# A four-stage image kernel: one move and one normalisation to ScalarE, loads and stores to other queues, a product in two column halves

## The chip, the cores and the metric

The kernel runs on one core of one Trainium2 chip. The metric is the device time of one execution in microseconds. All arithmetic is in fp32. TensorE, VectorE, ScalarE and GpSimd work in parallel, and each takes its own instructions in order; SyncE (SP in the profile) issues DMAs. The ScalarE queue can issue DMAs too.

## What is computed

An image x of 48 channels and 128 by 128 pixels passes through four layers. Each takes a group-normalised input (16 groups of 3 channels) and adds its result to x.

```python
# 0: attention over all 16384 pixels, one head of 48 channels
q, k, v = split(depthwise3x3(qkv_w @ gn(x)))
x = x + proj_w @ (softmax(l2norm(q) @ l2norm(k).T * temperature) @ v)
# 1: four recurrent sweeps (down, up, right, left), each row or column plus a 5-tap conv of the one before
x = x + sweeps(gn(x))
# 2: 8x8 patches: q and k are multiplied in the frequency domain, layer-normed, gated by v
q, k, v = split(depthwise3x3(w_hidden @ gn(x)))
x = x + w_out @ (v * layernorm(irfft2(rfft2(q) * rfft2(k)))) + b_out
# 3: selective scan over 4096 tokens (2x2 windows) of 192 features, 192 states
delta = softplus(softplus(tokens @ W_dt.T + b_dt) + b_dt)
h = exp(delta * A) * h + (delta * u) * B        # for every token
x = x + (h @ C + D * u) * sigmoid(1)
```

## The kernel before

**Attention** (`attend`) works on chunks of 512 queries (32 chunks) against 64 tiles of keys. For each tile, `scores` makes four products on TensorE (pass by pass, eight records, 64x64 positions of the array) and one exp on ScalarE (L48 `e<-s`); `sums` adds tile j into `acc`, two tiles behind (`BEHIND = 2`). TensorE and ScalarE run in an order written out by hand: the `InOrder` wrapper chains every instruction given to `act` or `pe` to the one before it, and all of these are recorded under its line, L48. VectorE is not chained in this stage. At the end of a chunk, `Finish` copies `acc` to `o` on ScalarE, adds the two halves into `both` on VectorE (L366), moves partitions 64 to 127 of it to a tile `second` (L368), adds (L370, `y`), takes the reciprocal of the row of sums (L373, `rec`) and spreads it over 48 partitions with three DMAs (L376, `recs`). `Finish.result` multiplies, adds the residual, takes statistics and stores the chunk; it stands after tile 6 of the next chunk in the order, and directly after the last chunk.

**Sweeps** begin with GpSimd memsets of borders of the image buffer (L592 to L608; the largest, L604, covers 32 partitions by 16512 elements), the group statistics (L71 to L87) and a ScalarE normalisation (L617).

**The patch stage** (`patch_conv`) works on 32 groups of four image rows in a software pipeline written out by hand for TensorE, ScalarE and VectorE. In the order of one round: `columns` (24 passes `pc`), `turn` of three groups back (four transposes `po<-ident,y`), `others`, `keys` (`f`), `back` of two groups back (`po<-k,gm`, then mean and difference on VectorE and a square on ScalarE), `leave` of three groups back (the product with `wout`, then bias and residual in one VectorE instruction), `gate` of two groups back (variance, root, multiplication on VectorE; three GpSimd multiplications and additions, L893 to L895), `queries` and `count`. The three kinds of `po` share two PSUM buffers.

**The scan** begins with `token_stats`, which leaves scale and offset in `so`. `scan` loads weights on two queues, makes `a = -exp(A_log)`, and prepares the first 1024 tokens in `first`: it normalises two parts of 512 tokens, projects them (`both`, whose accumulators are the two PSUM buffers named `dA`), runs softplus twice, and stores `rep` (delta and delta times u) and `yu` in DRAM. Activation functions that need another table make a load of 1.28 us (ACT_TABLE_LOAD). The main loop has 32 rounds a chunk of 1024 tokens, with three steps each. A step loads `du` and `dt` from `rep` on SP (L1484), multiplies on GpSimd (L1489, `h<-du,bt`), makes three exps on ScalarE (`dA<-dt,a`) and three scans on VectorE (L1496). TensorE contracts `h` with `cw` into `y`. The tiles `cw` are placed from `ct` by six ScalarE copies after `first`. Later chunks are prepared in small portions within the loop.

DMAs complete on eight semaphores that are used in turn over both queues; a DMA whose semaphore is still in use waits in its queue.

Of the kernel before, what the change touches and what calls it, by code (L numbers as in the profile page):

```python
# [19 lines left out]
F32 = mybir.dt.float32  # L20
F16 = mybir.dt.float16
AF = mybir.ActivationFunctionType
ALU = mybir.AluOpType
# [3 lines left out]
C = 48  # L27
H = W = 128
N = H * W
CH = 512  # L30
GAP = 49
SIGMOID_1 = 0.7310585786300049
# [63 lines left out]
def rows(ap, n=W):  # L96
    return ap.rearrange("c (r w) -> c r w", w=n)
# [209 lines left out]
@with_exitstack  # L307
def attend(ctx, tc, xq, k, v, x1, absT, st, ins):

    nc = tc.nc
    act, pe = InOrder(tc, nc.scalar), InOrder(tc, nc.tensor)
    NQ = N // CH
    KT = N // 2 // 128
    BEHIND = 2

    ep = ctx.enter_context(tc.tile_pool(name="l0_e", bufs=BEHIND + 3))  # L320
    sp = ctx.enter_context(tc.tile_pool(name="l0_b", bufs=2))
    ps_s = ctx.enter_context(tc.tile_pool(name="l0_ps", bufs=3, space=PSUM))
    ps_a = ctx.enter_context(tc.tile_pool(name="l0_pa", bufs=1, space=PSUM))


    sides = [slice(0, 64), slice(64, 128)]
    quarters = [(part, half, to) for part in sides for half, to in enumerate(sides)]

    def scores(c, j):
        s = ps_s.tile([128, 2, CH], F32, name="s")  # L330
        for part, half, _ in quarters:
            b = 64 * half
            pe.matmul(
                s[part, half, :],
                lhsT=k[b : b + GAP, j * 128 + part.start : j * 128 + part.stop],
                rhs=xq[b : b + GAP, c * CH : (c + 1) * CH],
                start=True,
                stop=True,
            )
        e = ep.tile([128, 2, CH], F32, name="e")  # L340
        act.activation(e, s, AF.Exp, scale=absT)
        return e

    def sums(acc, j, e):

        for part, half, to in quarters:
            pe.matmul(
                acc[to, part.start // 64, :],
                lhsT=v[part, half * KT + j, :],
                rhs=e[part, half, :],  # L350
                start=(j == 0),
                stop=(j == KT - 1),
            )

    class Finish:


        def __init__(self, c, acc):
            self.c = c
            self.cols = slice(c * CH, (c + 1) * CH)  # L360
            self.xres = sp.tile([C, CH], F32, name="xres")
            nc.sync.dma_start(self.xres, ins["x"][:, self.cols])
            o = sp.tile([128, 2, CH], F32, name="o")
            act.copy(o, acc)
            both = sp.tile([128, CH], F32, name="both")
            nc.vector.tensor_add(both, o[:, 0], o[:, 1])  # L366
            second = sp.tile([64, CH], F32, name="second")
            nc.vector.tensor_copy(second, both[64:128])  # L368
            self.y = sp.tile([64, CH], F32, name="y")
            nc.vector.tensor_add(self.y, both[0:64], second)  # L370

            rec = sp.tile([64, CH], F32, name="rec")
            nc.vector.reciprocal(rec[32:64], self.y[32:64])  # L373
            self.rec = sp.tile([C, CH], F32, name="recs")
            for i in range(0, C, 64 - C):
                nc.sync.dma_start(self.rec[i : i + 64 - C], rec[C:64])  # L376

        def result(self):
            y = self.y[0:C]
            nc.vector.tensor_mul(y, y, self.rec)  # L380
            nc.vector.tensor_add(xq[0:C, self.cols], y, self.xres)
            nc.vector.bn_stats(st[:, self.c, :], xq[0:C, self.cols])
            nc.sync.dma_start(x1[:, self.cols], xq[0:C, self.cols])

    waiting, finish, acc = [], None, None
    for c in range(NQ):
        for j in range(KT):
            waiting.append((c, j, scores(c, j)))

            if c and j == BEHIND:  # L390
                continue
            while len(waiting) > BEHIND:
                n, i, e = waiting.pop(0)
                if i == 0:
                    acc = ps_a.tile([128, 2, CH], F32, name="acc")
                sums(acc, i, e)
                if i == KT - 1:
                    finish = Finish(n, acc)
            if c and j == BEHIND + 4:
                finish.result()  # L400
    for n, i, e in waiting:
        sums(acc, i, e)
    Finish(NQ - 1, acc).result()


@with_exitstack
# [304 lines left out]
def patch_conv(ctx, tc, xq, other, x3, const, ins):  # L711

    nc = tc.nc
    act, pe, dve = (InOrder(tc, e) for e in (nc.scalar, nc.tensor, nc.vector))
    ident = const["ident"]
    C2, C6 = 2 * C, 6 * C
# [4 lines left out]
    sp = ctx.enter_context(tc.tile_pool(name="l2_s", bufs=2))  # L721
    ps_c = ctx.enter_context(tc.tile_pool(name="l2_pc", bufs=4, space=PSUM))
    ps_f = ctx.enter_context(tc.tile_pool(name="l2_pf", bufs=1, space=PSUM))
    ps_o = ctx.enter_context(tc.tile_pool(name="l2_po", bufs=2, space=PSUM))
# [18 lines left out]
    wout = wp.tile([C2, C], F32, name="wout")  # L743
    nc.sync.dma_start(wout, ins["l2_wout"])
    bout = wp.tile([C, 1], F32, name="bout")
# [158 lines left out]
        act.copy(yts[g], pt)  # L904

    def leave(g):
        pw = ps_o.tile([C, CH], F32, name="po")
        pe.matmul(
            pw, lhsT=wout, rhs=yts.pop(g).rearrange("c r w -> c (r w)"), start=True, stop=True
        )  # L910
        xc = xq[0:C, g * CH : (g + 1) * CH]
        dve.scalar_tensor_tensor(xc, pw, bout, xc, ALU.add, ALU.add)

    def count(g):
        dve.bn_stats(const["st"][:, g, :], xq[0:C, g * CH : (g + 1) * CH])
# [53 lines left out]
def scan(ctx, tc, x3, const, ins, out):  # L969
# [7 lines left out]
    nc = tc.nc  # L977
# [3 lines left out]
    C2 = 2 * C  # L981
# [26 lines left out]
    def load(name, shape, eng):  # L1008
        t = wp.tile(shape, F32, name=name)
        eng.dma_start(t, ins[f"l3_{name}"])  # L1010
        return t

    wdt = load("wdt", [C2, 2, 2, C2], nc.sync)
    bdt = load("bdt", [C2, 2], act)
    wb = load("wb", [C2, 2, 3, 128], nc.sync)
    bb = load("bb", [128, 3], act)
    wc = load("wc", [C2, 2, 3, 128], nc.sync)
    bc = load("bc", [128, 3], act)
    a = load("a", [128, 3, Q], nc.sync)
    dp = load("dp", [C2, 2], act)  # L1020
    sel = load("sel", [128, BK, 8], act)
    act.activation(a, a, AF.Exp)
    nc.vector.tensor_scalar_mul(a, a, -1.0)
    plus = ident[0:C2, 0:C2]
    minus = wp.tile([C2, C2], F32, name="minus")
    nc.scalar.mul(minus, plus, -1.0)
    sig = wp.tile([128, 128], F32, name="sig")
    nc.scalar.mul(sig, ident, SIGMOID_1)


    cw = wp.tile([128, 3, LC // BK, 2 * BK], F32, name="cw")
# [10 lines left out]
    def prepare(ci):  # L1042
# [9 lines left out]
        def first():  # L1052
# [8 lines left out]
            for part, x in enumerate(us):  # L1061
                xi = rows(const["x3"][:, part, :]).rearrange("c i (j b) -> c i j b", b=2)
                xo = x.rearrange("c b (i j) -> c i j b", j=64)
                if part == 0:
                    act.activation(
                        xo, xi, AF.Identity, bias=so[:, 1:2], scale=so[:, 0:1]
                    )
                else:
                    nc.vector.tensor_scalar(xo, xi, so[:, 0:1], so[:, 1:2], ALU.mult, ALU.add)

            def both(lhsT, m):
                t = ps_a.tile([128, LC], F32, name="dA")
# [19 lines left out]
            for again in range(2):  # L1092
                for b in range(2):
                    split(b, dd[:, b, 0] if again else both(lambda i: wdt[:, i, b, :], C2))
                for b in range(2):
                    act.activation(e[:, b], e[:, b], AF.Exp, scale=-1.0)
                    nc.vector.tensor_scalar_add(w[:, b], e[:, b], 1.0)
                for b in range(2):
                    act.activation(ln[:, b], w[:, b], AF.Ln)

                    nc.vector.scalar_tensor_tensor(
                        w[:, b], w[:, b], 1.0, e[:, b], ALU.subtract, ALU.subtract
                    )
                    nc.vector.tensor_sub(e[:, b], dd[:, b, 1], w[:, b])
                if again == 0:
                    for k in range(2):
                        take_both(bt[:, k], both(lambda i: wb[:, i, k, :], 128), bb[:, k : k + 1])
                for b in range(2):
                    nc.vector.tensor_add(dd[:, b, 0], e[:, b], ln[:, b])
            take_both(bt[:, 2], both(lambda i: wb[:, i, 2, :], 128), bb[:, 2:3])  # L1110
            for b in range(2):
                for part, x in enumerate(us):
                    cols = slice(part * L, (part + 1) * L)
                    nc.vector.tensor_mul(dd[:, b, 1, cols], dd[:, b, 0, cols], x[:, b, :])
                for i in range(2):
                    half = slice(i * C, (i + 1) * C)
                    nc.sync.dma_start(rep_by[i][:, b], dd[half, b])
            for k in (2, 0, 1):
                take_both(ct[:, k], both(lambda i: wc[:, i, k, :], 128), bc[:, k : k + 1])
            for part, x in enumerate(us):  # L1120
# [2 lines left out]
                        w[:, b, part * L : (part + 1) * L], x[:, b], AF.Copy, scale=dp[:, b : b + 1]  # L1123
                    )
            for i in range(2):
                nc.sync.dma_start(yu_by[i][:, :, 0:LC], w[i * C : (i + 1) * C])

        def accumulator():
            return ps_p.tile([128, L], F32, name="pp")
# [609 lines left out]
```

## Time and profile before

| what | value |
|---|---|
| median of three runs | 7612.05 us (7606.72 to 7613.94) |
| the profiled execution | 7615.01 us |
| its span, first to last instruction | 7613.2 us |
| granted TensorE clock, mean | 0.885 |
| busy TensorE, VectorE, ScalarE, GpSimd | 80%, 45%, 58%, 37% |
| attention, first convolution to last chunk | 0 to about 3778 us |
| sweeps, with their start | 3778 to about 4490 us |
| patch stage, with its start | 4490 to about 4884 us |
| scan, with its start | 4884 to 7613 us |

The page gives busy time for each engine and a chain that ended last, followed back from the last instruction to what released each step. Since the four stages follow one another, a share of the whole span says little of a seam between two of them; the timeline of a window shows each instruction with its start, its duration, and in brackets the idle time of its engine before it with what ended that idle time. A busy TensorE is modelled at its ends, and work on GpSimd is rough.

### The profile page before, as it was taken

Reading aid. Unit: us, or ns where it says so; the run is one execution under the profiler, and the core shown is the slowest. Engines: PE = TensorE matmul, PEld = TensorE weight load, DVE = VectorE, ACT = ScalarE, POOL = GpSimd, SP = SyncE. Lnnn points to the kernel's source line nnn. Section 1 sums busy time; section 2 is a strip of 40 time slices with the busy share of each in tenths; the row PEclk is TensorE's granted clock in tenths of the full one; section 3 lists DMA queues with packets and bytes.
Section 4 is the critical chain, followed back from the end, with each engine's and each line's share of the span. In section 5 each row is a group of like instructions: output and inputs, shape, how many; then the busy total and the mean of one; then the engine's idle time right before and its main releaser. Section 6 shows DMA issues by size and latency. Waiting matters only on the chain.

```text
span 7613.2 us, 203122 instructions
## 1 busy us (share of the span) xinstructions
PE 6126.1 (80%) x93692; PEld 3179.7 (42%) x93692; DVE 3405.3 (45%) x2498; ACT 4389.0 (58%) x4835; POOL 2791.8 (37%) x574
## 2 busy tenths in 40 slices
PE   7999999999999999999888889745545545554555
PEld 3333333333333333333367765334434433434444
DVE  8300000000000000000122234499999999999998
ACT  2566666666666666666525003367666666666665
POOL 0000000000000000000000022299999999999998
PEclk9999999999999999999999999867767766676667
DMA  3000000000000000000000011166656666666776
GB/s 66 9 3 4 4 3 4 4 4 3 4 4 4 3 4 4 3 4 4 3 1 17 1 32 37 31 163 169 159 160 163 157 160 153 167 162 162 177 182 149
DMA packets 182349, 484.83 MB, mean 64 GB/s; under 512 B 35859, under 2 KB 67778, under 8 KB 179506
## 3 DMA queue, kind: packets, MB, share of 16 engines
q1 hardware_dynamic: 175167, 466.19, 24.2%
q8 instruction: 734, 12.03, 0.7%
q10 hardware_dynamic: 6323, 5.59, 0.3%
q14 instruction: 125, 1.02, 0.0%
HBM read 428.03 MB, written 22.02 MB: 59 GB/s over the span
## 4 chain that ended last, share of the span: by engine, by line
PE 60%; DVE 24%; issue 6%; POOL 3%; ACT 2%; DMA 2%; SPq 0%; DVEq 0%; ACTq 0%; POOLq 0%
PE s L48 23%; PE acc L48 23%; DVE h L1496 21%; PE p L672 6%; POOL h L1489 3%; PE pc L48 3%; PE y L48 3%; DVE xb L48 1%; DVE xa L48 1%; PE po L48 1%; DMA du<-rep 1%; PE f L48 1%; ACT dA L48 1%; PE pp L48 0%; ACT L48 0%
## 5 line engine op out<-in xcount | busy, mean ns | idle before, releaser
L48 ACT ACTIVATE e<-s,absT 128x1024 f32<-128x1024 f32 x2048 | 2279.3, 1115 | 1217.2 <-PE s L48 1217.2
L1489 POOL TENSOR_TENSOR h<-du,bt 128x3072 f32<-128x3072 f32 (+1 forms) x386 | 2559.5, 6675 | 96.7 <-DMA du<-rep 69.7
L48 PE MATMUL s<-xa,xb 49*64 49x512 f32 x16384 | 2137.3, 589 | 10.6 <-DVE xb L271 10.6
L48 PE MATMUL acc<-e,xb 64*64 64x512 f32 x16384 | 2135.4, 588 | 0.0
L1496 DVE TENSOR_TENSOR_SCAN h<-dA,carry,h 128x1024 f32<-128x1024 f32 x864 | 1940.2, 2322 | 41.0 <-ACT dA L48 27.3
L48 ACT ACTIVATE dA<-dt,a 128x1024 f32<-128x1024 f32 x1152 | 1287.2, 1118 | 877.4 <-DVE h L1496 865.2
L48 PE MATMUL y<-h,cw 128*32 128x48 f32 x49152 | 891.7, 244 | 956.6 <-issue 501.6
L366 DVE TENSOR_TENSOR both<-o 128x512 f32<-128x512 f32 x32 | 22.1, 692 | 3192.8 <-ACT o L48 3192.8
L608 POOL MEMSET xa<- 48x128 f32 x1 | 0.3, 327 | 3523.5 <-PE acc L48 3523.5
L48 PEld LDWEIGHTS y<-h,cw 128*32 128x32 f32 x49152 | 801.1, 139 | 1081.7 <-issue 664.8
L48 PEld LDWEIGHTS s<-xa,xb 49*64 49x64 f32 x16384 | 650.5, 132 | 1123.2 <-issue 583.4
L48 PEld LDWEIGHTS acc<-e,xb 64*64 64x64 f32 x16384 | 649.7, 132 | 1112.4 <-issue 1089.5
L1496 DVE TENSOR_TENSOR_SCAN h<-dA,h 128x1024 f32<-128x1024 f32 x288 | 636.0, 2270 | 41.3 <-ACT dA L48 30.4
L48 PE MATMUL yz<-ev,sel 128*8 128x48 f32 x4096 | 192.4, 260 | 270.6 <-ACT ev L48 269.0
L48 PEld LDWEIGHTS yz<-ev,sel 128*8 128x8 f32 x4096 | 162.2, 106 | 327.8 <-ACT ev L48 306.4
L672 PE MATMUL p<-xb,l_w 112*112 112x129 f32 x1524 | 236.4, 291 | 41.8 <-DVE xb L48 41.7
L672 PE MATMUL p<-xa,l_w 112*112 112x129 f32 x1524 | 232.2, 288 | 41.8 <-DVE xa L48 41.8
L693 POOL TENSOR_TENSOR xb<-xb,xa 48x2048 f32<-48x2048 f32 (+2 forms) x10 | 44.6, 4459 | 561.7 <-DVE xa L48 561.7
L672 PEld LDWEIGHTS p<-xb,l_w 112*112 112x112 f32 x1524 | 184.3, 179 | 93.6 <-DVE xb L48 93.6
L655 ACT COPY xa<-xb 48x128 f32<-48x128 f32 x256 | 107.3, 419 | 197.2 <-issue 138.8
L672 PEld LDWEIGHTS p<-xa,l_w 112*112 112x112 f32 x1524 | 180.6, 176 | 93.2 <-DVE xa L48 93.2
L48 PE MATMUL pc<-wt,xa 128*128 128x288 f32 x768 | 199.7, 418 | 7.5 <-DMA xa<-xa 7.5
(187 smaller groups left out, 3345.7 us busy)
## 6 DMA issues: line engine op xcount, KB each, us to landing
du<-rep SPq DMA_DIRECT2D x768, 256.0 KB
dt<-rep SPq DMA_DIRECT2D x768, 256.0 KB
rep<-dd SPq DMA_DIRECT2D x24, 192.0 KB
yd<-ys ACTq DMA_DIRECT2D x256, 12.0 KB
rest<-xa SPq DMA_DIRECT2D x90, 38.0 KB
band<-band SPq DMA_DIRECT2D x8, 414.4 KB
xa<-in_x_dram SPq DMA_DIRECT2D x8, 384.0 KB
rest<-band SPq DMA_DIRECT2D x96, 32.0 KB
```

What stands on the lines that cost most here:

```text
L48: ins = method(*args, **kwargs).ins
L366: nc.vector.tensor_add(both, o[:, 0], o[:, 1])
L608: nc.gpsimd.memset(b[64:K, lines, E + W - 1 : E + W], 0.0)
L655: nc.scalar.copy(u[at : at + C, :, y], t[0:C, E + h, E : E + W])
L672: nc.tensor.matmul(p, lhsT=w[0:K, which, i, :], rhs=state[0:K, 2 * i : 2 * i + L], start=False, stop=(i == 2),)
L693: nc.gpsimd.tensor_add(xr, xr, u[0:C, x : x + xr.shape[2], E : E + H].rearrange("c w h -> c h w"),)
L1489: nc.gpsimd.tensor_mul(h[:, p, ks], du.unsqueeze(1).to_broadcast([128, ks.stop - ks.start, LC]), r["bt"][:, ks],)
L1496: nc.vector.tensor_tensor_scan(h[:, p, k, :], dA, h[:, p, k, :], carry[:, i, k : k + 1] if ci else 0.0, ALU.mult, ALU.add,)
```

## The change

In `attend`, the move of the upper half of `both` goes from VectorE to ScalarE. A new method `divide` holds it with the addition, the reciprocal and its DMAs; it stands after tile 4 of the next chunk, and `result` after tile 8 in place of tile 6. In `patch_conv`, the output product is made in two halves of 256 columns, which go to PSUM partitions 0 to 47 and 64 to 111; two VectorE instructions add bias and residual. In `scan`, all loads go on SyncE; the exp of `a`, its sign and two scaled identities go to a function `tables` that is called in the middle of the first preparation; both first normalisations are on ScalarE; of the four first `rep` stores, two go on the ScalarE queue, and so do the two first `yu` stores.

```diff
-            both = sp.tile([128, CH], F32, name="both")
-            nc.vector.tensor_add(both, o[:, 0], o[:, 1])
+            self.both = sp.tile([128, CH], F32, name="both")
+            nc.vector.tensor_add(self.both, o[:, 0], o[:, 1])
+
+        def divide(self):
             second = sp.tile([64, CH], F32, name="second")
-            nc.vector.tensor_copy(second, both[64:128])
+            act.copy(second, self.both[64:128])
             self.y = sp.tile([64, CH], F32, name="y")
-            nc.vector.tensor_add(self.y, both[0:64], second)
+            nc.vector.tensor_add(self.y, self.both[0:64], second)
...
-            if c and j == BEHIND + 4:
+            if c and j == BEHIND + 2:
+                finish.divide()
+            if c and j == BEHIND + 6:
                 finish.result()
...
-    Finish(NQ - 1, acc).result()
+    finish = Finish(NQ - 1, acc)
+    finish.divide()
+    finish.result()
...
     def leave(g):
-        pw = ps_o.tile([C, CH], F32, name="po")
-        pe.matmul(
-            pw, lhsT=wout, rhs=yts.pop(g).rearrange("c r w -> c (r w)"), start=True, stop=True
-        )
-        xc = xq[0:C, g * CH : (g + 1) * CH]
-        dve.scalar_tensor_tensor(xc, pw, bout, xc, ALU.add, ALU.add)
+        pw = ps_o.tile([64 + C, 2, W], F32, name="po")
+        y = yts.pop(g)
+        for n in range(2):
+            pe.matmul(
+                pw[64 * n : 64 * n + C], lhsT=wout, rhs=y[:, 2 * n : 2 * n + 2], start=True, stop=True
+            )
+        for n in range(2):
+            xc = rows(xq[0:C, g * CH + 2 * n * W : g * CH + (2 * n + 2) * W])
+            dve.scalar_tensor_tensor(xc, pw[64 * n : 64 * n + C], bout, xc, ALU.add, ALU.add)
...
-    bdt = load("bdt", [C2, 2], act)
+    bdt = load("bdt", [C2, 2], nc.sync)
...
-    act.activation(a, a, AF.Exp)
-    nc.vector.tensor_scalar_mul(a, a, -1.0)
...
-    nc.scalar.mul(minus, plus, -1.0)
-    nc.scalar.mul(sig, ident, SIGMOID_1)
+
+    def tables():
+        act.activation(a, a, AF.Exp)
+        nc.vector.tensor_scalar_mul(a, a, -1.0)
+        act.mul(minus, plus, -1.0)
+        act.mul(sig, ident, SIGMOID_1)
...
-                if part == 0:
-                    act.activation(
-                        xo, xi, AF.Identity, bias=so[:, 1:2], scale=so[:, 0:1]
-                    )
-                else:
-                    nc.vector.tensor_scalar(xo, xi, so[:, 0:1], so[:, 1:2], ALU.mult, ALU.add)
+                act.activation(xo, xi, AF.Identity, bias=so[:, 1:2], scale=so[:, 0:1])
...
                 if again == 0:
+                    tables()
                     for k in range(2):
                         take_both(bt[:, k], both(lambda i: wb[:, i, k, :], 128), bb[:, k : k + 1])
...
-                    nc.sync.dma_start(rep_by[i][:, b], dd[half, b])
+                    (act if i else nc.sync).dma_start(rep_by[i][:, b], dd[half, b])
...
-                nc.sync.dma_start(yu_by[i][:, :, 0:LC], w[i * C : (i + 1) * C])
+                act.dma_start(yu_by[i][:, :, 0:LC], w[i * C : (i + 1) * C])
```

The loads of bb, bc, dp and sel change as that of bdt.

More of the change, by code (lines that the diff above doesn't have):

```diff
@@ L1013, in scan @@
     wdt = load("wdt", [C2, 2, 2, C2], nc.sync)
-    bdt = load("bdt", [C2, 2], act)
+    bdt = load("bdt", [C2, 2], nc.sync)
     wb = load("wb", [C2, 2, 3, 128], nc.sync)
-    bb = load("bb", [128, 3], act)
+    bb = load("bb", [128, 3], nc.sync)
     wc = load("wc", [C2, 2, 3, 128], nc.sync)
-    bc = load("bc", [128, 3], act)
+    bc = load("bc", [128, 3], nc.sync)
     a = load("a", [128, 3, Q], nc.sync)
-    dp = load("dp", [C2, 2], act)
-    sel = load("sel", [128, BK, 8], act)
-    act.activation(a, a, AF.Exp)
-    nc.vector.tensor_scalar_mul(a, a, -1.0)
+    dp = load("dp", [C2, 2], nc.sync)
+    sel = load("sel", [128, BK, 8], nc.sync)
     plus = ident[0:C2, 0:C2]
     minus = wp.tile([C2, C2], F32, name="minus")
-    nc.scalar.mul(minus, plus, -1.0)
     sig = wp.tile([128, 128], F32, name="sig")
-    nc.scalar.mul(sig, ident, SIGMOID_1)
+    def tables():
[3 more added lines that the diff above has]
+        act.mul(sig, ident, SIGMOID_1)
     cw = wp.tile([128, 3, LC // BK, 2 * BK], F32, name="cw")
```

## The prediction

> **What bounds the kernel now.** I read the chain of waits first (section 4 of the page), because one core runs four stages in a row and a busy share is an average over them.
>
> ```profile
> PE 60%; DVE 24%; issue 6%; POOL 3%; ACT 2%; DMA 2%; SPq 0%; DVEq 0%; ACTq 0%; POOLq 0%
> ```
>
> TensorE carries attention (to 3778 us), the sweeps and the patch stage; VectorE carries the scan from 4954 us. ScalarE and the queues hold little, so what is moved to them matters only where stages meet. The timeline at the end of attention shows such a place:
>
> ```profile
> 3778.83 13.91 POOL L604 MEMSET xb<- 32x16512 f32 x1
> 3779.45 0.69 DVE L366 TENSOR_TENSOR both<-o 128x512 f32<-128x512 f32 x1 [97.35 <-ACT o L48]
> 3780.17 12.85 DVE L368 COPY second<-both 64x512 f32<-64x512 f32 x1
> 3793.05 0.69 DVE L370 TENSOR_TENSOR y<-both,second 64x512 f32<-64x512 f32 x1
> ```
>
> Columns: start, duration, engine, line. `second` takes 12.85 us, and ends just after the GpSimd memset ends (3792.74). By tile, the other 31 copies take 0.42. The chain of waits in this window runs through it: `second` 12.86, then rec 3.35, the rec DMA, the statistics, and the sweeps' first normalisation at 3809.71.
>
> The patch stage repeats every 10.886 us; its chain is TensorE alone. One period in the timeline:
>
> ```profile
> 4665.10 0.87 PE L48 MATMUL po<-k,gm 128*64 128x384 f32 x4
> 4665.80 1.02 PE L48 MATMUL po<-yt,wout 96*48 96x512 f32 x2
> 4666.75 0.88 PE L48 MATMUL f<-qkv,fm 64*64 64x384 f32 x8
> ...
> 4667.35 0.73 DVE L48 SCALAR_TENSOR_TENSOR xb<-po,bout,xb 48x512 f32<-48x512 f32 x1
> ...
> 4668.08 0.55 DVE L48 TENSOR_REDUCE var<-sq 128x4 f32<-128x384 f32 x1
> ...
> 4672.18 0.99 POOL L895 TENSOR_TENSOR y<-y,qkv 128x384 f32<-128x384 f32 x1
> ...
> 4673.48 0.60 PE L48 MATMUL po<-ident,y 128*96 128x128 f32 x4
> ```
>
> The output product holds TensorE from 4665.80 to 4666.75. But L895 ends at 4673.17 and the transposes that need it start at 4673.48: the loop through VectorE, ScalarE and GpSimd is nearly as long as TensorE's. The scan's start, same view:
>
> ```profile
> 4888.17 5.22 POOL L1032 MEMSET cw<- 128x6144 f32 x1 [8.51 <-DVE gn_rstd L87]
> ...
> 4889.16 5.13 DVE L1069 TENSOR_SCALAR xn<-x_first,so 96x1024 f32<-96x1024 f32 x1
> ...
> 4894.29 0.44 ACT L48 ACTIVATE a<-a 128x288 f32<-128x288 f32 x1 [2.04 <-DMA a<-in_l_a_dram]
> 4894.64 2.15 ACT L48 ACTIVATE xn<-x_first,so 96x1024 f32<-96x1024 f32 x1
> ...
> 4919.56 1.28 ACT L48 ACT_TABLE_LOAD   x1
> ...
> 4940.55 0.79 SPq L1126 DMA_DIRECT2D yu<-h  x2
> 4941.45 2.76 SPq L1484 DMA_DIRECT2D du<-rep  x2
> ...
> 4953.79 6.65 DVE L1496 TENSOR_TENSOR_SCAN h<-dA,h 128x1024 f32<-128x1024 f32 x3 [19.23 <-ACT dA L48]
> ```
>
> The statistics are ready at 4889.1, yet ScalarE first issues five loads and waits for `a`; VectorE's half again sits beside a memset. Later the du loads stand in SP's queue behind the yu stores.
>
> **What the Trainium skill says.** "SBUF — State Buffer", "Who interferes with whom": VectorE's copy and tensor_scalar can take the port pair shared with GpSimd and then block for its whole instruction; a tensor_tensor contends only with a GpSimd instruction that reads. The trace agrees: 12.85 and 5.13 us beside memsets, but `both` 0.69 beside the same memset. "ScalarE: Activation LUTs", "Table sets: the hidden batching unit": cheap functions stand in every set. Agreed: the second pair of Abs (4917.26) runs after Ln without a load; the load comes with Exp. "TensorE: Matmul & The Clock Gate", "Part 3: Packing small matmuls — row/col tiling": products at different column positions overlap. Agreed: the four `gm` passes start in pairs, 0.37 and 0.32 us apart, so they occupy 0.70, not the 1.28 that four passes of 0.32 would. "DMA: Bandwidth & Descriptors", "Issuing engines are not separate DMA queues": a second queue saves only issue time; SP's four rep stores take 3.59 us to issue.
>
> **Attention, -12.2 us.** `second` becomes a ScalarE copy; nearest row, xa<-xa 64x512: 0.61. At the last chunk: `both` ends 3780.14, the copy ends 3780.8, y starts 3780.85 instead of 3793.05. Everything after it moves by 12.2: y, rec (3.34), three DMAs, result, statistics. What is late next is GpSimd, whose last border memset ends at 3794.6; the first ScalarE normalisation of the sweeps would come at 3797.5, so 2.9 us spare. Rec under the memset: at 106 us a reciprocal overlapped one and kept 3.35. Bounds: 9.3 (if the borders end 2.9 later) to 12.4.
>
> The other 31 chunk ends: the copy stands in ScalarE's order after the exp of tile 4. TensorE needs 1.72 us a tile and ScalarE is busy 1.11, so 0.60 is idle; in the chunk end at 478 us `both` is done at 479.74 and tile 4's exp ends at 483.27, so the copy waits for nothing and ends as the next scores arrive (483.88). The exps queued behind it are at most 0.1 late; TensorE works two tiles behind, and VectorE's y, rec, result come some 4 us later, where it idles about 97 us per chunk. Cost 0; bounds 0 to +3 (0.1 x 31).
>
> **Patch stage, -3.4 us.** Two passes of 512 columns (0.43 each, 0.95 with the change-over) become four passes of 256 at two column positions; like `gm`, two pass times of 0.21 and change-overs, about 0.53. TensorE's own loop: 10.89 - 0.42 = 10.47. VectorE: two tensor_tensor rows of the scan's start (1024 columns 1.216, 512 columns 0.680) give 1.05 ns a column, so a half move costs 0.73 - 0.27 = 0.47; consecutive moves overlap 0.08, so the second ends at 4668.18 instead of 4668.06, and `var`, which now waits for `sq` (4668.06), starts about 0.035 later. The other loop: from `gm` to L895's end 8.07, weight load 0.065 + 0.13, from the transposes to the next `gm` 2.51: 10.775, with 0.035 10.81. This is the bound after the change, not 10.47. Gain 0.076 x 29 full periods = 2.2. In the drain, two slow-clock passes of 0.85 shrink once (-0.85, +0.1 for VectorE) and a 0.27 wait and some issue go: 1.2 more. Bounds: if the weight load needn't be waited for, 0.2 a period, 7; the full 0.42, 13; if the halves run one after another with 0.1 each for change-over, +3.
>
> **Scan start, -6.0 us.** Removed from ScalarE ahead of the first normalisation: five DMA issues (4888.13 to 4890.43), two multiplications, a table load, the wait for `a`, its Exp. Both normalisations now go on ScalarE, 2.06 each: 4889.16, 4891.2, 4893.3. TensorE starts on the first half at 4891.3 instead of 4896.84: -5.5; its four slow passes (0.85 each) cover the second half, and wdt landed at 4890.35. SP's four loads become nine, 0.4 each; wdt stays first, bdt is next, and `a`, dp and sel are needed 15 us or more later. Next, Exp's table load lies on the path: +1.28. The moved Exp(a) with its load, minus and sig (2.3 in all) fill ScalarE's idle 2.88 before L1109's result; VectorE's sign change of `a` is on the path: +0.31. The load at 4919.56 is gone, as Exp's set is active: -1.28. So bt 2 comes at 4921.0: -5.1 or so.
>
> Then the added waits. ScalarE's share of the rep stores waits for VectorE's products (4928.2 and 4929.4) and issues in 0.4 to 1.6 each; **ct 2, before at 4927.08, is queued behind them**: 4930.5. TensorE's last projection needs ct 2's accumulator: start 4931.6, then 3.4 to 6.0 by its clock. Then ct 1 1.05, dp 2.45, two yu issues 0.8 to 2, six cw copies 6.3, table load 1.28, exp 1.2: VectorE's first scan at 4948.2 to 4951.9 against 4953.79. I take -3.5. The du loads on SP lose the yu stores ahead of them: rep rows land 4 us after issue, so du can be issued from 4932.5 and, at 6 us to land as now, starts GpSimd by 4938.5 to 4942, not 4949.34. GpSimd then leads, and VectorE's 2.47 idle at 4962.92 (put down to GpSimd) goes: -2.5. Later scan idle is ScalarE's table loads and GpSimd's wait for dd, which stay. Bounds: 0 to -12.
>
> Sum: 12.2 + 3.4 + 6.0 = 21.6. The profiled execution took 7615.01 us (span 7613.2 and 1.8 around it), so 7593.4; that is 3.0 above the median of the three runs, so **7590**.
>
> **Rivals.** *More*: GpSimd's earlier start, not VectorE's, sets the scan (-11), and the patch loop yields its full 13: -36, 7576. For it: early in the scan the chain goes through GpSimd's h. Against: ScalarE's cw copies come first. *Less*: the halves don't run side by side, or the period stays because the loop through GpSimd binds, and the rep stores on ScalarE eat the scan's gain: attention alone, 7600. For it: the 0.3 us slack, and ct 2 behind a wait. *Slower*: the copy at 31 chunk ends holds ScalarE's queue until `both`, or longer, so that exps come late and TensorE stalls. A stall of 1.2 us would cost 37, net +16: 7628. It decides from 21.6/31 = 0.7 us per chunk end; against it stand the 3.5 us for which `both` is done before.
>
> **How the numbers follow.** Forecast 0.66 (own range 7584 to 7597), more 0.14, less 0.16, slower 0.04. About 0.2% or 15 us is what this measurement tells from no change: faster by more 0.83, within 0.13, slower 0.04. Range 7576 to 7603: down to the rival with more, and up past attention alone.
>
> **What would show it.** `second` as 32 ScalarE copies near 0.6, y 0.7 us after `both` at the last chunk; scores and exps still 1.72 us apart there. Patch period 10.8, with `wout` near 0.5 and TensorE idle some 0.3 on L895 (right), or 10.47 (loop wrong), or 10.9 and over (halves wrong). First dA product 2.2 us after `so`; GpSimd's first h well ahead of VectorE's first scan; no 2.47 idle at the second step. I'm wrong if the sweeps start less than 9 us earlier, or if the scan starts no earlier relative to `so`.

## The result and the profile after

The changed kernel takes 7597.65 us (median of 19 runs, 7591.17 to 7604.73); the kernel before, in the same session, 7615.82 (19 runs, 7606.72 to 7625.98). The ratio is 0.9975, 95% interval 0.9968 to 0.9982: faster by 0.25%, some 19 us (14 to 24). The forecast was 21.6 us from a base of 7612.05; from 7615.82 it would have read 7594.2.

The spans are 7613.2 and 7595.7 us, 17.5 apart. The table cuts both profiled executions at the same landmarks (a landmark is the start of an instruction, but for the sweeps' last product, `so` and the last scan, which count by their end).

| stretch | before | after | difference |
|---|---|---|---|
| start to the sweeps' first normalisation | 3809.71 | 3797.56 | -12.15 |
| from there to the sweeps' last product | 673.83 | 671.23 | -2.60 |
| to the patch stage's first product | 12.53 | 12.57 | +0.04 |
| from there to scale and offset of the scan (`so`) | 393.05 | 391.84 | -1.21 |
| from there to VectorE's first scan | 64.67 | 62.69 | -1.98 |
| first to last scan | 2639.27 | 2639.88 | +0.61 |
| last scan to the end | 20.14 | 19.92 | -0.22 |

The chain of waits of the changed kernel, by engine (section 4 of its page):

```profile
PE 58%; DVE 24%; issue 7%; POOL 4%; ACT 2%; DMA 1%; SPq 0%; DVEq 0%; POOLq 0%; ACTq 0%
```

TensorE lost two points, GpSimd won one: `y` of L899 to L901 has joined the chain. The end of attention in the timeline (start, duration, engine, line), below it the first normalisation of the kernel before:

```profile
3779.53 0.69 DVE L366 TENSOR_TENSOR both<-o 128x512 f32<-128x512 f32 x1 [93.66 <-ACT o L48]
...
3779.87 13.91 POOL L610 MEMSET xb<- 32x16512 f32 x1
3780.25 0.62 ACT L48 COPY second<-both 64x512 f32<-64x512 f32 x1 [0.76 <-DVE both L366]
3780.90 0.68 DVE L372 TENSOR_TENSOR y<-both,second 64x512 f32<-64x512 f32 x1 [0.68 <-ACT second L48]
3781.62 3.34 DVE L375 RECIPROCAL rec<-y 32x512 f32<-32x512 f32 x1
...
3795.16 0.32 POOL L614 MEMSET xb<- 48x128 f32 x1
...
3797.56 1.24 ACT L623 ACTIVATE xb<-xa,off,gn_rstd 48x1024 f32<-48x1024 f32 x1 [0.47 <-DVE off L619]
```

```profile
3809.71 39.22 ACT L617 ACTIVATE xb<-xa,off,gn_rstd 48x1024 f32<-48x1024 f32 x32 [0.47 <-DVE off L613]
```

`second` runs beside the same long memset and keeps 0.62 us, as in all 32 places (616 to 619 ns). The last border ends at 3795.48, 2.1 us before the first normalisation, so GpSimd has not become the late one. One period of the patch stage, same view:

```profile
4661.42 0.87 PE L48 MATMUL po<-k,gm 128*64 128x384 f32 x4
...
4662.12 0.60 PE L48 MATMUL po<-yt,wout 96*48 96x256 f32 x4
...
4663.68 0.97 DVE L48 SCALAR_TENSOR_TENSOR xb<-po,bout,xb 48x256 f32<-48x256 f32 x2
...
4664.56 0.54 DVE L48 TENSOR_REDUCE var<-sq 128x4 f32<-128x384 f32 x1
...
4668.65 1.00 POOL L901 TENSOR_TENSOR y<-y,qkv 128x384 f32<-128x384 f32 x1
4669.70 0.40 PEld L48 LDWEIGHTS po<-ident,y 128*96 128x96 f32 x4 [0.61 <-POOL y L901]
4669.71 0.64 PE L48 MATMUL po<-ident,y 128*96 128x128 f32 x4 [0.16 <-POOL y L901]
```

The product's four passes now show as 0.60 where two passes showed as 1.02, and the bracket after the transposes is new: TensorE waits for L901. The chain of waits from 4660 to 4674 us names the same loop:

```profile
by line: PE po L48 16.3%; PE pc L48 13.6%; PE f L48 11.5%; DVE mu L48 10.7%; DVE y L48 8.1%; POOL y L900 7.2%; POOL y L901 7.2%; POOL y L899 7.2%; DVE xb L48 6.2%; DVE var L48 6.0%; issue 4.5%; ACT var L48 1.5%; DVEq L48 0.3%; POOLq L899 0.
```

The period, a mean from one L901 to the one 25 groups later, is 10.842 us against 10.886. The scan's start, timeline, and below it four lines of the kernel before:

```profile
4873.23 4.13 ACT L48 ACTIVATE xn<-x_first,so 96x1024 f32<-96x1024 f32 x2 [1.20 <-DVE so L975]
...
4875.46 9.70 PE L48 MATMUL dA<-xn,wdt 96*96 96x512 f32 x16 [2.46 <-ACT xn L48]
...
4906.59 3.70 PE L48 MATMUL dA<-xn,wc 96*128 96x512 f32 x8 [0.83 <-ACT bt L48]
...
4912.76 1.56 ACTq L48 DMA_DIRECT2D rep<-h  x2
4912.86 1.42 SPq L1125 DMA_DIRECT2D rep<-h  x2
4914.42 2.12 ACT L48 ACTIVATE ct<-dA,bc 128x1024 f32<-128x1024 f32 x2 [7.89 <-DVE h L1122]
...
4915.59 6.70 PE L48 MATMUL dA<-xn,wc 96*128 96x512 f32 x8 [5.30 <-ACT ct L48]
...
4924.70 26.80 POOL L1497 TENSOR_TENSOR h<-du,bt 128x1024 f32<-128x1024 f32 x6 [47.22 <-DMA du<-rep]
...
4935.89 11.02 DVE L1504 TENSOR_TENSOR_SCAN h<-dA,h 128x1024 f32<-128x1024 f32 x5 [21.96 <-ACT dA L48]
```

```profile
4896.84 9.18 PE L48 MATMUL dA<-xn,wdt 96*96 96x512 f32 x16 [7.91 <-ACT xn L48]
...
4927.08 1.10 ACT L48 ACTIVATE ct<-dA,bc 128x1024 f32<-128x1024 f32 x1
4927.23 9.37 PE L48 MATMUL dA<-xn,wc 96*128 96x512 f32 x16 [6.67 <-ACT bt L48]
...
4962.92 2.29 DVE L1496 TENSOR_TENSOR_SCAN h<-dA,h 128x1024 f32<-128x1024 f32 x1 [2.47 <-POOL h L1489]
```

TensorE starts 2.3 us after `so` (4873.20), where it took 7.7. Then comes the cost. ScalarE computes nothing for 7.89 us: it waits until VectorE has made the rows of `rep`, issues its two stores (the last 1.6 us of the gap), and only then makes the `ct` for which TensorE waits. Before, this `ct` followed at once. GpSimd starts 51.5 us after `so` instead of 60.2, and VectorE scans without the pause of 2.47 us at the second step.

### The profile page after: what moved, and what is told of

It reads as the page before. It is cut to its first block, busy times and chain, and to the rows that moved or that the text cites. A ratio compares the mean times of both kernels' runs of the same rounds, so it can differ in the third digit from the quotient of the medians.

```text
span 7595.7 us, 203249 instructions
## 1 busy us (share of the span) xinstructions
PE 6125.8 (81%) x93756; PEld 3162.8 (42%) x93756; DVE 3378.7 (44%) x2497; ACT 4410.3 (58%) x4868; POOL 2792.3 (37%) x574
## 3 DMA queue, kind: packets, MB, share of 16 engines
q14 instruction: 125, 1.02, 0.0%
## 4 chain that ended last, share of the span: by engine, by line
PE 58%; DVE 24%; issue 7%; POOL 4%; ACT 2%; DMA 1%; SPq 0%; DVEq 0%; POOLq 0%; ACTq 0%
PE s L48 23%; PE acc L48 23%; DVE h L1504 20%; PE p L678 6%; POOL h L1497 3%; PE y L48 2%; DVE xb L48 1%; DVE xa L48 1%; DMA du<-rep 1%; PE pp L48 1%; PE pc L48 1%; PE po L48 1%; ACT dA L48 1%; DVE y L48 0%; POOL y L901 0%
## 5 line engine op out<-in xcount | busy, mean ns | idle before, releaser
L678 PE MATMUL p<-xb,l_w 112*112 112x129 f32 x1524 | 233.6, 289 | 42.6 <-DVE xb L48 42.5
L699 POOL TENSOR_TENSOR xb<-xb,xa 48x2048 f32<-48x2048 f32 (+2 forms) x10 | 44.7, 4465 | 559.0 <-DVE xa L48 559.0
```

The source lines that it names most:

```text
L678: nc.tensor.matmul(p, lhsT=w[0:K, which, i, :], rhs=state[0:K, 2 * i : 2 * i + L], start=False, stop=(i == 2),)
L699: nc.gpsimd.tensor_add(xr, xr, u[0:C, x : x + xr.shape[2], E : E + H].rearrange("c w h -> c h w"),)
```

## Experiments: one part at a time

Three kernels hold one part each. The first, attention alone (its other parts as in the kernel before):

```diff
-            nc.vector.tensor_copy(second, both[64:128])
+            act.copy(second, self.both[64:128])
...
+            if c and j == BEHIND + 2:
+                finish.divide()
...
```

> Only the move of `second` to ScalarE, the rest as before. Theory (port held by the border memset): the last `second` takes 0.62, the sweeps' first normalisation comes 12.2 us earlier, and since TensorE then idles some 12 us less, the first sweep rows run at the slow clock for fewer rows: about 2.6 more, as in the changed kernel's profile; in all -13 to -16 us. Rival (the 31 copies inside the chunks cost exps): the scores and exps of a chunk end come over 1.72 us apart, and the total moves by less than 9. The patch period stays 10.886 us and the scan starts 64.7 us after the scale and offset are ready.

Measured: 7601.85 us against 7619.31, ratio 0.998 (0.9972 to 0.9987), so 15 us (10 to 21). `second` takes 0.62 and the sweeps' first normalisation comes at 3798.20. In the changed kernel, which has the same attention, a chunk end reads so in the timeline:

```profile
482.24 1.12 ACT L48 ACTIVATE e<-s,absT 128x1024 f32<-128x1024 f32 x1 [1.12 <-PE s L48]
482.79 1.04 PE L48 MATMUL s<-xa,xb 49*64 49x512 f32 x8
483.38 0.62 ACT L48 COPY second<-both 64x512 f32<-64x512 f32 x1
483.65 1.04 PE L48 MATMUL acc<-e,xb 64*64 64x512 f32 x8
484.02 1.11 ACT L48 ACTIVATE e<-s,absT 128x1024 f32<-128x1024 f32 x1
...
484.51 1.04 PE L48 MATMUL s<-xa,xb 49*64 49x512 f32 x8
```

The copy fills ScalarE's gap between two exps, and the scores stay 1.72 us apart. The slower rival (exps held at 31 chunk ends) is out: the last chunk's `o` comes at 3778.48 in the changed kernel and at 3778.95 in this one, against 3778.40.

The patch stage alone:

```diff
-        pw = ps_o.tile([C, CH], F32, name="po")
+        pw = ps_o.tile([64 + C, 2, W], F32, name="po")
...
```

> Only the output product in two column halves. Theory (the loop through VectorE, ScalarE and GpSimd binds): the period goes from 10.886 to 10.82 us and not to 10.47, TensorE waits before the transposes, total -2 to -3 us, which the timed rounds can hardly tell from nothing. Rival (TensorE alone binds): period 10.47, -13 us.

Measured: 7620.04 us, ratio 1.0004 (0.9996 to 1.0012), no change that can be told from none. The period is 10.821 us instead of 10.886, and the 29 full periods together are 1.5 us shorter, which is far inside the runs' scatter.

The scan's start alone:

```diff
-    bdt = load("bdt", [C2, 2], act)
+    bdt = load("bdt", [C2, 2], nc.sync)
...
-                nc.vector.tensor_scalar(xo, xi, so[:, 0:1], so[:, 1:2], ALU.mult, ALU.add)
...
-            nc.sync.dma_start(yu_by[i][:, :, 0:LC], w[i * C : (i + 1) * C])
+            act.dma_start(yu_by[i][:, :, 0:LC], w[i * C : (i + 1) * C])
```

> Only the edits of the scan's start. Theory: VectorE's first scan comes 62 to 63 us after scale and offset are ready (before 64.7), the 2.5 us wait at the second step is gone, so -4.5 us there; what the rest of the scan keeps of it depends on how later preparation falls, so the total is -1 to -5 us. Rival (GpSimd's earlier start sets the scan's end): -8 us or more.

Measured: 7611.11 us, ratio 0.9988 (0.9982 to 0.9995): 9 us (4 to 14). From `so`, TensorE starts at 2.3, GpSimd at 51.55, the first scan comes at 63.2, and the second step's scans 6.57 after the first instead of 9.12. The expectation named 1 to 5 us, its rival 8 or more; the interval reaches into both. In the profiled execution the last scan starts 2699.8 us after `so`, which is 1.8 to 9.6 us earlier than in the five profiles with the old start. So attention gives most of the gain, and the scan the rest, with a size that these runs leave wide.

## Experiments: is it the shared memset?

The kernel before, its copy left on VectorE, with the long memset cut into 16 pieces:

```diff
-        nc.gpsimd.memset(b[32:64, lines, inside], 1.0)
+        for at in range(lines.start, lines.stop, 8):
+            nc.gpsimd.memset(b[32:64, at : at + 8, inside], 1.0)
```

> The kernel before, but each GpSimd memset of 32 partitions by 16512 elements is cut into 16 of eight lines; `second` stays on VectorE. Theory (VectorE's copy waits for the GpSimd instruction that holds the shared port, and only for that one): the last `second` takes about 0.4 to 1.5 us instead of 12.85, the sweeps start 11 to 12 us earlier, total -12 to -15. Rival 1 (the copy waits until GpSimd's whole row of memsets is done): still some 13 us, total 0. Rival 2 (the move to ScalarE mattered for another reason than the port): `second` as long as before.

Measured: 7600.23 us, ratio 0.9974 (0.9964 to 0.9983). Timeline of its chunk end:

```profile
3780.33 1.28 DVE L368 COPY second<-both 64x512 f32<-64x512 f32 x1
3780.38 0.95 POOL L605 MEMSET xb<- 32x1032 f32 x1
```

The copy now ends 0.28 us after the piece beside it, as it ended 0.28 us after the whole memset before, and takes 1.28; it does not wait for GpSimd's further memsets, which go on to 3783.2. (By the record the copy starts 0.05 us ahead of the piece, but GpSimd's records are rough.) That is what the Trainium skill says in "SBUF — State Buffer", "Who interferes with whom": whoever has the shared pair keeps it for its whole instruction. One edit on GpSimd alone thus gives what the move to ScalarE gives. But the cut also did something that its text does not show: 15 of the 16 pieces ran earlier, one at 6.6 us and the others between 3732 and 3780 us, most of them released by a product of attention, while the uncut memset started only at 3778.83. So one piece alone was left to fall beside the copy, and how a copy fares beside sixteen pieces in a row was not tried.

The cut gives something more: TensorE's first product of the sweeps follows the normalisation by 2.6 us, where it waits 7.2 in both kernels; two normalised blocks are done by then, where it was six. First the kernel before, then the pieces:

```profile
3816.89 0.74 PE L647 MATMUL p<-xb,l_wi 112*112 112x129 f32 x2 [9.40 <-ACT xb L617]
```

```profile
3801.24 0.74 PE L648 MATMUL p<-xb,l_wi 112*112 112x129 f32 x2 [4.86 <-ACT xb L618]
```

No run shows why. In the time of the whole kernel the extra 4.5 us cannot be told from the move to ScalarE (7600.23 against 7601.85 us).

## Experiments: what bounds the patch stage

The addition of `beta`, one of GpSimd's three instructions, is left out of the changed kernel and of the kernel before (`beta` is zero in the inputs):

```diff
         nc.gpsimd.tensor_mul(y, y, over_rows(gamma))
-        nc.gpsimd.tensor_add(y, y, over_rows(beta))
         nc.gpsimd.tensor_mul(y, y, qkv.pop(g)[:, :, 2 * C2 :])
```

> The changed kernel without the GpSimd addition of beta in the patch stage (left out; beta is zero in the inputs). Theory (the loop through VectorE, ScalarE and GpSimd binds the changed kernel at 10.82 to 10.84 us a period): that loop is 1.07 shorter, so TensorE's own 10.47 binds and the patch stage is 10 us shorter than in the changed kernel; against the kernel before about -28 us. Rival (something in TensorE's queue holds the period): period still 10.8, total as the changed kernel, -18.

> The kernel before without the addition of beta (left out; beta is zero in the inputs). Theory (TensorE binds the kernel before at 10.886): the period stays 10.886 although GpSimd's part is 1.07 shorter. Rival (the loop already bound before): period 10.6 or less.

Measured: the changed kernel without `beta` has a period of 10.467 us and takes 7585.65 us, ratio 0.9962 (0.9948 to 0.9975), or 29 us less than the kernel before, as expected. The kernel before without `beta` keeps 10.886 in its one profiled execution. TensorE therefore binds before the change, and the loop through VectorE, ScalarE and GpSimd after it; the 10.47 of the prediction is TensorE's own period.

## Experiments: where the scan's gain stops

First the queues: the four `rep` stores back on SyncE, then `rep` and `yu` both.

```diff
-                    (act if i else nc.sync).dma_start(rep_by[i][:, b], dd[half, b])
+                    nc.sync.dma_start(rep_by[i][:, b], dd[half, b])
```

> The changed kernel with all four first rep stores back on SyncE (the yu stores stay on the ScalarE queue). Theory (ct 2 behind the rep stores in ScalarE's order costs what the earlier start gained): ct 2 follows bt 2 at once, TensorE's last projection follows without a gap at 0.43 a pass, VectorE's first scan comes about 55 us after scale and offset (62.7 in the changed kernel), GpSimd's first h at about 51.5; total 5 to 7 us less than the changed kernel, -23 to -25 against before. Rival (the two queues are what brings du early): the first scan is limited by du and comes no earlier than 62.

> The changed kernel with all first rep and yu stores back on SyncE. Theory: ct 2 is free as above, but du stands behind the yu stores: GpSimd's first h about 53.5 us after scale and offset and VectorE's first scan about 58; total 3 to 5 us less than the changed kernel, 2 to 3 more than with the rep stores alone on SyncE. Rival (the store queues gain as intended): the first scan later than 62.7, total more than the changed kernel.

Measured: 7598.51 us, ratio 0.9978 (0.9969 to 0.9987), and 7595.97 us, ratio 0.9974 (0.9965 to 0.9984). Neither can be told from the changed kernel; of the 5 to 7 us expected of the first nothing shows (they would lie at the edge of its interval), the 3 to 5 expected of the second lie within its interval. Yet the first scan comes 57.1 and 58.3 us after `so` instead of 62.7. With `rep` on SyncE the timeline shows why half of that is lost at once:

```profile
4912.52 1.11 ACT L48 ACTIVATE ct<-dA,bc 128x1024 f32<-128x1024 f32 x1 [2.96 <-DVE h L1117]
...
4914.89 3.59 SPq L1125 DMA_DIRECT2D rep<-h  x4
...
4928.41 26.80 POOL L1497 TENSOR_TENSOR h<-du,bt 128x1024 f32<-128x1024 f32 x6 [48.53 <-DMA du<-rep]
...
4932.70 6.65 DVE L1504 TENSOR_TENSOR_SCAN h<-dA,h 128x1024 f32<-128x1024 f32 x3 [16.75 <-ACT dA L48]
...
4942.00 11.09 DVE L1504 TENSOR_TENSOR_SCAN h<-dA,h 128x1024 f32<-128x1024 f32 x5 [2.65 <-POOL h L1497]
```

`ct` no longer stands behind the stores, but four stores in one queue take SyncE 3.59 us and end 2.5 us after the last of their rows (with two queues 0.4), GpSimd starts 1.3 later, and VectorE idles 2.65 at its second step. At the tenth step the lead of 5.6 is down to 2.0 (119.6 against 121.6 us after `so`), and the last scan comes later than in the changed kernel's profile. That end is weak evidence: these two profiled executions took 6.2 and 12.6 us more than the medians of their kernels.

Next the two halves of the start. The second half of the normalisation back on VectorE, and, in another kernel, ScalarE's five loads and `tables` back ahead of the normalisation:

```diff
+                if part == 0:
+                    act.activation(xo, xi, AF.Identity, bias=so[:, 1:2], scale=so[:, 0:1])
+                else:
+                    nc.vector.tensor_scalar(xo, xi, so[:, 0:1], so[:, 1:2], ALU.mult, ALU.add)
```

> The changed kernel with the second half of the scan's first normalisation back on VectorE. Theory that the gain at the scan's start comes from the loads and tables that left ScalarE's way ahead of the first half, and not from the engine of the second half: the first dA product stays 2.3 us after the scale is ready, TensorE's four slow passes (3.4 us) cover VectorE's half, which ends 5.1 us after it beside GpSimd's memset, the first scan stays at 62 to 63.5 us, and the time is the changed kernel's within 2 us. Rival: VectorE's half is late for the fifth pass and its engine starts the step sizes later, so that the first scan comes at 64 us or later and half the part's gain goes (+2 us).

```diff
-    bdt = load("bdt", [C2, 2], nc.sync)
+    bdt = load("bdt", [C2, 2], act)
...
+    tables()
...
                 if again == 0:
-                    tables()
```

> The changed kernel with ScalarE's five loads and the four operations on a, minus and sig back ahead of the first normalisation. Theory that these hold the start: the first normalisation begins about 5 us after the scale instead of at once, the first dA product 7.5 us after it or more (both halves now on ScalarE), and the first scan at 66 to 68 us instead of 62.7; the time is 2 to 5 us above the changed kernel's, less if the scan gives back what it starts late. Rival: ScalarE waits later for VectorE's step sizes and TensorE's projections anyway (5.3 us idle before the last projection), so that the first scan moves by under 1.5 us and the time not at all.

Measured: 7598.56 us, ratio 0.9977 (0.9968 to 0.9986), first scan at 62.7 us after `so`: the engine of the second half is worth nothing that shows. With loads and tables early: 7604.05 us, ratio 0.9985 (0.9979 to 0.9992), first dA product at 7.4, first scan at 68.0. The first scan is 5.3 us later, the median 5.5 above its neighbour's; the two intervals overlap a little. So the way cleared on ScalarE is worth 5.3 at the first scan, and the `rep` stores on ScalarE's queue cost 5.6 there (62.7 against 57.1).

Last, a theory on why an earlier start does not reach the end: GpSimd's multiplication by ScalarE's copy of the step sizes (`with_u`) waits for ScalarE at VectorE's pace and throws GpSimd's lead away. It goes one slot later:

```diff
-                [with_u, b_(0)],
-                [take_b(0), b_(1)],
-                [store, take_b(1), b_(2)],
-                [take_b(2)],
+                [b_(0)],
+                [with_u, take_b(0), b_(1)],
+                [take_b(1), b_(2)],
+                [store, take_b(2)],
```

> The changed kernel with GpSimd's multiplication by ScalarE's copy of the step sizes (with_u) moved from the first to the second slot of each step's last list, so that the first multiplication by B comes ahead of it. Theory that GpSimd's early start in the scan is thrown away because this multiplication waits for ScalarE's copy at VectorE's pace: those waits, 32.3 us over the scan of the changed kernel with one of 10.6 us, fall to under 5 us, the 5.8 us for which VectorE then waits for GpSimd go, and the kernel takes 10 to 15 us less than the changed kernel (ratio to the kernel before 0.9955 to 0.9962). Rival that the scan is bound by VectorE and TensorE's sums together and the wait only shows slack: the wait moves to another line (GpSimd waits for TensorE's y or for a buffer), and the time is the changed kernel's within 2 us (0.9974 to 0.998). Third: the multiplication by u comes late for VectorE, the first scan moves later by 0.5 to 1.5 us a chunk and the time is longer than the changed kernel's by up to 10 us.

Measured: 7598.28 us, ratio 0.9976 (0.9968 to 0.9984). The waits of GpSimd in the scan of this kernel (engine, line, what it waited for: us in total, times, longest):

```profile
POOL h L1497 <- DMA du<-rep: 66.6, 12, 46.8
POOL dd L1221 <- ACT dd L48: 25.5, 5, 9.1
POOL h L1497 <- PE y L48: 23.8, 18, 3.3
```

The wait for `dd` fell from 32.3 to 25.5 only, the wait for `y` rose from 17.8 to 23.8, and VectorE waits for GpSimd 25.9 us in all, where it waited 23.9 in the changed kernel. One slot was not enough to remove the wait, so the theory in its full form was not tested, but what it promised of this edit, 10 to 15 us, failed; the rival that the wait only moves to another line fits.

## A version that beats both

The changed kernel with the memset in pieces, `with_u` later, and the products of v with `gamma` and `beta` formed ahead, so that two GpSimd instructions follow the normalisation instead of three (the first two edits are shown above):

```diff
-        nc.gpsimd.tensor_mul(y, y, over_rows(gamma))
-        nc.gpsimd.tensor_add(y, y, over_rows(beta))
-        nc.gpsimd.tensor_mul(y, y, qkv.pop(g)[:, :, 2 * C2 :])
+        vg, vb = gates.pop(g)
+        nc.gpsimd.tensor_mul(y, y, vg)
+        nc.gpsimd.tensor_add(y, y, vb)
...
+    def weigh(g):
+        t = qkv.pop(g)
+        gates[g] = [t[:, :, n * C2 : (n + 1) * C2] for n in range(2)]
+        for to, by in zip(gates[g], (gamma, beta)):
+            nc.gpsimd.tensor_mul(to, t[:, :, 2 * C2 :], over_rows(by))
...
             queries(g - 1)
+            weigh(g - 1)
```

> The changed kernel with three edits: the borders' memset in 16 pieces; GpSimd's products of v with gamma and with beta formed ahead, so that two GpSimd instructions instead of three follow the normalisation in the patch stage; with_u one slot later in the scan. Theory: the patch loop falls to TensorE's own period, 10.47 us instead of 10.84 (about -11 us, as in the run without beta), the first sweep product follows the normalisation by 2.6 us (-3 to -4.5 us), and the scan gives what the run with with_u alone gives (0 to -15 us): together 7565 to 7585 us, ratio to the kernel before 0.9935 to 0.996. Rival for the patch part: the two products ahead take the shared GpSimd time that the third instruction took, the loop through GpSimd stays at 10.8, and only the memset's -4 remains (ratio about 0.997).

Measured: 7587.23 us (7579.97 to 7591.52), ratio 0.9962 (0.9949 to 0.9976), 11 us below the kernel with `with_u` late in the same session. The two ratios' intervals meet at their edge, but of the single times only one of each kernel cross (7591.52 and 7590.51). The 7565 to 7585 us that were expected are missed by 2 us: the patch stage and the first sweep product came as expected, the scan gave nothing more that shows. The profiled execution is the fastest of the five. One period of its patch stage, timeline:

```profile
4654.17 1.00 POOL L911 TENSOR_TENSOR qkv<-qkv,beta 128x384 f32<-128x384 f32 x1 [3.64 <-ACT qkv L48]
...
4656.14 1.00 POOL L911 TENSOR_TENSOR qkv<-qkv,gamma 128x384 f32<-128x384 f32 x1 [0.97 <-PE f L48]
...
4658.92 1.00 POOL L901 TENSOR_TENSOR y<-y,qkv 128x384 f32<-128x384 f32 x1 [1.79 <-DVE y L48]
...
4660.00 0.99 POOL L902 TENSOR_TENSOR y<-y,qkv 128x384 f32<-128x384 f32 x1
4661.88 0.38 PE L48 MATMUL po<-ident,y 128*96 128x128 f32 x2
```

GpSimd does four instructions instead of three, but the two ahead run where it idled; the last ends at 4660.99, 0.9 us before the transposes, which no longer wait. The period is 10.466, TensorE's own. The chain of waits of that window (4650 to 4662 us) holds TensorE alone:

```profile
by line: PE pc L48 74.1%; PE po L48 13.9%; PE f L48 13.4%
```

## Why the prediction held, point by point

**Attention, -12.2: right**, in mechanism and size. The first normalisation moved by 12.15; only_attention and memset_pieces reach the same place in two ways. GpSimd had 2.1 us to spare where 2.9 was estimated, and the 31 inner copies cost nothing that shows. (The lower bound of 9.3 counts the spare time the wrong way: with 2.9 us to spare, borders that end 2.9 later cost nothing.) The Trainium skill's "SBUF — State Buffer", "Who interferes with whom", also says that ScalarE waits for no one at SBUF: 0.62 us beside the memset, as without it.

**Sweeps: no term in the prediction, and 2.6 us of luck.** The granted clock reached full speed 11.4 us after the first normalisation in the changed kernel's profile, 19.6 us after it in the profile before. Until then the sweep's rows stand 2.0 us apart, afterwards 1.3: one such slow step in one case, five in the other. The eight profiles with identical attention and sweeps have one to seven, full speed comes at 10.9 to 23.4 us, and from first normalisation to last product they take from 670.96 (attention alone) to 677.88 us (`rep` and `yu` on SyncE). The kernel before, with 673.83, lies in the middle. So 2.6 of the 17.5 us between the two spans are not the change's, and the reason that the expectation for attention alone gives, that TensorE idles less, does not decide it: four of the eight have four to seven slow steps.

**Patch, -3.4: right mechanism, term too large.** The loop through GpSimd does bind. Its usual period, 10.82 to 10.83 us, is close to the forecast 10.81, but in each of the seven profiles with the halves one period takes 11.16 to 11.18, which lifts the mean to 10.842 here; in that period VectorE starts a subtraction 0.36 us late, and no run shows why. Together the 29 full periods are 1.3 to 1.5 us shorter, not 2.2. In the drain the last product shrinks by the forecast 0.85 (1.94 to 1.09), but VectorE's two halves take 0.24 more than the one move (0.98 against 0.74), where 0.1 was put: after the last L901 the drain is 0.6 shorter in all seven. From the first L901 (L895 before) to `so` the seven take 344.9 to 345.5 us, four profiles of the old form with `beta` 347.4 to 347.6, so 2.2 in all. The table shows 1.21 because the stage's start, up to the first L901, took 1.0 more in this pair; over the eleven profiles it varies from 44.7 to 46.9 us.

**Scan start, -6.0: right at its beginning, too large at its end.** TensorE's start (-5.5 forecast, 7.72 to 2.27 measured), GpSimd's (49.4 to 52.9 us after `so` forecast, 51.5 measured) and the 2.47 idle that goes are as forecast. ct 2 behind the stores is too: TensorE's last projection was to start 42.5 us after `so` and started at 42.4. The mis-sized term is that projection's duration, put at 3.4 to 6.0 us with a middle value: it took 6.70, since TensorE had idled 5.30 us for `ct` and restarted slow, at a granted clock of 0.55. Where it idled 0.83, in the projection before, eight equal passes took 3.70 at a granted clock of 1.00. The Trainium skill has this in "TensorE: Matmul & The Clock Gate", "Part 1: The HAM clock gate": slow after an idle window of about 3.4 us. So the first scan moved by 2.0, at the slow end of the forecast 1.9 to 5.6, not by 3.5.

What the prediction left out is that the scan need not keep an early start. With the 2.55 at the second step, the changed kernel is 4.5 ahead there, and 5.4 at the tenth step; at the last scan 1.4 in this pair. Five profiles with the old start begin their last scan 2701.6 to 2709.4 us after `so` (mean 2704.2); the changed kernel, the one without `beta`, the scan alone and the normalisation on VectorE, 2699.8 to 2703.2 (mean 2701.0). That is 3.2 kept of 4.5, and less than the scatter among the old ones. By the medians, the scan alone brings 4 to 14. The parts' ratios make up the whole within their intervals. Which wait takes the lead back, where it goes, stays open: neither the order of the stores (two kernels) nor a later `with_u` brought a gain that the medians can tell.

**The sum and the base.** The forecast took 21.6 from a median of three runs, 7612.05, which the later 19 runs put at 7615.82: these 3.8 us are half of the distance from 7590 to 7597.65. The rest is a gain of 18.2 us by the medians instead of 21.6. The measured time lies in the stated range of 7576 to 7603, but 0.65 us above the forecast's own 7584 to 7597. The total alone does not tell the forecast from its rival "less", attention alone: the intervals 14 to 24 us and 10 to 21 overlap. Part of that rival came true, since the patch loop binds and the `rep` stores on ScalarE cost 5.6 us at the first scan. What speaks for the forecast is the scan alone, which is faster by 4 to 14, and the patch stage's 2.2 us in the traces.

## What to carry to other kernels

A long instruction that shares a port with another engine can cost a short one all that is left of its length, here 12.4 of 13.91 us; it can be cured from either side, by moving the short one or by cutting the long one, which also lets its pieces run as soon as each is free to. Where a loop of several engines is nearly as long as the busiest engine's own, shortening the engine yields only the difference, and the next step is to take work out of the loop's path, even at the price of more work beside it. A store that an in-order engine issues while its data are still late delays everything behind it on that engine, and an idle TensorE adds a slow restart to the delay.

## What was not expected of the hardware

- After 5.30 us without work, TensorE ran seven of eight passes of 512 columns slow: 6.70 us instead of 3.70. The granted clock was half from 4914.84 to 4921.66 us. At the scan's start six such passes stood 0.85 us apart before the spacing fell to 0.43.
- Cutting one GpSimd memset of 13.91 us into 16 of 0.95 changed not only VectorE's wait but also when TensorE starts: after two normalised blocks instead of six, 4.5 us earlier.
- Two queues take four stores in 1.56 us, one queue in 3.59; yet the kernel's ratio is 0.9975 in one case and 0.9978 in the other.
